# Position terms of an attention block: weights as windows of one small table on chip instead of tables from DRAM, heads interleaved, last terms in later turns

## The chip, the cores and the metric

The kernel runs on one core of a Trainium2 chip. The metric is the device time of one execution in microseconds (us). Before the change the median of three runs is 3649.41 us (3647.57 to 3650.12). PE is the matrix engine (PEld its weight loads), DVE the vector engine, ACT the scalar engine, POOL the GpSimd engine, and SP the engine that issues most of the DMAs. SBUF is the on-chip memory of 128 rows (partitions), PSUM the memory that PE writes its products to.

## The reference, cut to what matters

The program is a chain of four layers over an image of 48 x 48 positions with 768 channels: an attention block with an MLP, a spectral mixing layer, a scan layer, a second spectral layer. Only the attention block bears on the change:

```python
qkv = xn.reshape(B, H * W, C) @ qkv_w + qkv_b
...
attn = jnp.einsum('bqc,bkc->bqk', q * scale, k)
coords = jnp.arange(H)[:, None] - jnp.arange(H)[None, :] + (H - 1)
Rh = rel_pos_h[coords]
Rw = rel_pos_w[coords]
r_q = q.reshape(B * nh, H, W, hd)
rel_h = jnp.einsum('bhwc,hkc->bhwk', r_q, Rh)
rel_w = jnp.einsum('bhwc,wkc->bhwk', r_q, Rw)
attn = (attn.reshape(B * nh, H, W, H, W) + rel_h[:, :, :, :, None] + rel_w[:, :, :, None, :]).reshape(B * nh, H * W, H * W)
attn = jax.nn.softmax(attn, axis=-1)
out = jnp.einsum('bqk,bkc->bqc', attn, v)
```

There are 12 heads of 64 channels and 2304 positions. For a query in row h, `rel_h` is its 64 channels times 48 vectors, the 48 neighbouring rows of `rel_pos_h` (95 x 64) that start at a place which depends on h. `rel_w` is the same with the query's column w and `rel_pos_w`. So each of the 48 rows and 48 columns has its own 64 x 48 weights, and they are windows of one 64 x 95 array.

## The kernel before

Everything is float32. Two heads share the 128 rows of SBUF (`P`): head s of a pair has rows 64s to 64s+63. A matmul for both at once needs weights with zeros where the other head's channels stand. The host builds them: `relD` holds for each row and column a 128 x 96 block, columns 0 to 47 for the first head and 48 to 95 for the second, in groups of four positions (192 KB). The product has 96 rows, 0 to 47 of the first head and 48 to 95 of the second.

The qkv stage (`qkv_phase`, L241) works through the positions in three super-blocks of 768 (`sb`). For each it makes v (`v_rows`, L290, seven products by `rows_in_seven`) and then q and k for six pairs of heads (`q_and_k`, L328, seven products each with the weights `wqk`, 1344 KB, loaded from the scratch `wqk_d` by `load_qk`, L303). k, q and v go to scratch in DRAM.

The position terms of a super-block are a list of steps (`position_terms`, L439), 12 for rows (`rel_h`) and, except for the last super-block, 12 for columns (`rel_w`). Each step has a load and a run. `advance` (L492) keeps up to three loads ahead of the run; the runs are woven between the matmuls of q and k (L384) and of the next super-block's v (`between`, L502). A load issues one table of `relD` on SP's queue (`tables`, L433, four buffers); for rows it also has POOL copy q so that the positions of an image row stand side by side (`qh`, one buffer, L477 to L479). A run is four matmuls (L465, or L203 in `terms_w`) and `split_terms` (L186), in which ACT rounds the product to float32r and DVE subtracts for the rest. After four row steps, and after twelve column steps, two stores write the rows of the two heads to `rh_d` and `rw_d` (`store`, L446 to L448, on SP): 576 KB each for rh, 1728 KB each for rw.

The last super-block's column terms are made inside the attention stage, by the generator `last_terms_w` (L208): one load of q from scratch into part of `oT` (L217, 2304 KB), twelve products (L203), each with a table loaded three ahead in four buffers (L220 to L230), and stores at the end (L237). The attention stage (`attention_bounded`, L592) goes through 180 turns of three key tiles: scores (L629 products, L639 bias from `bt`), exp on ACT (L641), a running sum on DVE (L649), and every second turn the values (L660) of the two turns before; each six turns the row sums (L668), their reciprocal on DVE (L670) and the output (L676). Products of last terms share one PSUM bank (tag `rs`) with the row sums. Where they stand is written out by hand: one ahead of the values in the turns of `mid`, one after the values in the turns of `end` (L690):

```python
mid, end = {2, 3, 4, 5, 7, 8, 9, 10, 11, 13}, {8, 10}
```

Row sums come in turns 6 and 12. Beside the turns runs `weight_sums`, which loads weights of later stages on SP (`pw0b`, `pw1b`, ...), adds them on POOL (L134 to L137) and stores the sums; its tiles come from the pool of the exp results.

The order of SP's queue is the order of the program: an issue that waits for a free buffer holds all behind it. `relT`, the 64 x 2 x 95 array with both windows' sources, is also loaded (L413 to L415), for a bound on the scores (L422).

Of the kernel before, what the change touches and what calls it, by code (L numbers as in the profile page):

```python
# [20 lines left out]
P = 128  # L21
G = 48
# [170 lines left out]

def terms_w(nc, d, q, high, low, g, ps):


    R = 2 * G
    ps = ps[:R, :TB]
    pv = ps.rearrange("p (c b w h) -> p c b w h", c=NC, b=2, w=4)
    q6 = q.rearrange("p c b (j w h) -> p c b j w h", j=KJ, w=KTW)  # L200
    j, w0 = divmod(4 * g, KTW)
    for i in range(4):
        nc.tensor.matmul(pv[:, :, :, i, :], lhsT=d[:, i, :], rhs=q6[:, :, :, j, w0 + i, :], start=True, stop=True)  # L203
    cols = slice(j * P + w0 * KTH, j * P + (w0 + 4) * KTH)
    split_terms(nc, ps.rearrange("p (c b t) -> p c b t", c=NC, b=2), high[:R, :, :, cols], [(v[:R, :, :, cols], rows) for v, rows in low])


def last_terms_w(nc, oT, pw, pool, psum, q_d, rel_d, rw_d):  # L208
# [8 lines left out]
    nc.sync.dma_start(q.rearrange("p c b t -> p c (b t)"), q_d.rearrange("(c p) t -> p c t", p=P)[:, :, sb * ts : (sb + 1) * ts])  # L217
    tables = []

    def load(g):  # L220
        d = pool.tile([P, 4, 2 * G], F32, tag="relD", name=f"relDl_{g}", bufs=4)
        nc.sync.dma_start(d, rel_d[1, g])
        tables.append(d)

    for g in range(3):
        load(g)
    yield
    for g in range(G // 4):
        if g + 3 < G // 4:
            load(g + 3)  # L230
        terms_w(nc, tables.pop(0), q, high, low, g, psum(f"rwl_{g}"))
        if g == G // 4 - 1:
            for c0, c1 in ((0, 1), (1, NC2), (NC2, NC)):
                for s in range(2):
                    rows = slice(s * G, (s + 1) * G)
                    for n, v in enumerate((high[rows, c0:c1], low[c0 // NC2][0][rows, c0 % NC2 : (c1 - 1) % NC2 + 1])):
                        nc.sync.dma_start(rw_d[s, :, n, sb, c0 * ts : c1 * ts], v.bitcast(F32).rearrange("k c b t -> k (c b t)"))  # L237
        yield


def qkv_phase(tc, ident, x, qkv_w, qkv_b, relT, rel_d, ln_g, ln_b, q_d, k_d, v_d, rw_d, rh_d, wqk_d, wv_d, flag, home, ahead):  # L241

# [17 lines left out]
    with (  # L260
# [139 lines left out]
        with tc.tile_pool(name="qkv_v0", bufs=1, side="right") as vp:  # L400
# [11 lines left out]
            kb = kp.tile([P, NC], F32, tag="kb", name="kb")  # L412
            rel = qp.tile([P, 2, 2 * G - 1], F32, tag="rel", name="rel")  # L413
            for s in range(2):
                nc.sync.dma_start(rel[s * HD : (s + 1) * HD], relT)  # L415
            qms, kms = (qp.tile([P, NC, NSB], F32, tag=n, name=n) for n in ("qms", "kms"))
# [4 lines left out]
            rm = qp.tile([P, 2], F32, tag="rm", name="rm")  # L421
            V.tensor_reduce(rm, rel, axis=AX.X, op=ALU.max, apply_absolute_value=True)  # L422
            pz = qp.tile([P, 2, NC], F32, tag="pz", name="pz")
# [6 lines left out]
        with tc.tile_pool(name="qkv_o", bufs=1, side="right") as op:  # L430
            R = 2 * G

            def tables(which, g, n):  # L433

                d = qp.tile([P, 4, R], F32, tag="relD", name=f"relD_{which}_{g}_{n}", bufs=4)
                nc.sync.dma_start(d, rel_d[which, g])
                return d

            def position_terms(sb, q):  # L439
# [6 lines left out]
                def store(d, at, cols):  # L446
                    for s in range(2):
                        nc.sync.dma_start(d[s, :, :, sb, cols], at[s * G : (s + 1) * G].bitcast(F32).rearrange("k n c b t -> k n (c b t)"))  # L448

                def rel_w(g):  # L450
                    if g == 0:
                        tiles["rw"] = op.tile([P, KP, NC, 2, TB], F32R, tag="rw", name=f"rw_{sb}")
                    at = tiles["rw"]
                    terms_w(nc, tiles.pop(("w", g)), q, at[:, 0], [(at[:, 1], slice(0, NC))], g, pm.tile([P, 512], F32, tag="m", name=f"rw_{sb}_{g}"))
                    if g == G // 4 - 1:
                        store(rw_d, at, slice(0, NC * TS))

                def rel_h(cp, n, hh):

                    if (n, hh) == (0, 0):  # L460
                        tiles["rh"] = op.tile([P, KP, 2, 2, TB], F32R, tag="rh", name=f"rh_{sb}_{cp}")
                    (d, by_row), at = tiles.pop(("h", cp, n, hh)), tiles["rh"]
                    ps = pm.tile([P, 512], F32, tag="m", name=f"rh_{sb}_{cp}_{n}_{hh}")
                    for i in range(4):
                        nc.tensor.matmul(ps[:R, i * 2 * G : (i + 1) * 2 * G], lhsT=d[:, i, :], rhs=by_row[:, i], start=True, stop=True)  # L465
# [6 lines left out]
                def load(key, *args):  # L472
                    name = "_".join(str(k) for k in (sb, *key))
                    tiles[key] = tables(*args, name)
                    if key[0] == "h":
                        cp, n, hh = key[1:]
                        by_row = op.tile([P, 4, 2, KJ, KTW], F32, tag="qh", name=f"qh_{name}", bufs=1)  # L477
                        for c in range(2):
                            nc.gpsimd.tensor_copy(by_row[:, :, c], q6[:, 2 * cp + c, n, :, :, 4 * hh : 4 * hh + 4].rearrange("p j w h -> p h j w"))  # L479
                        tiles[key] = tiles[key], by_row.rearrange("p h c j w -> p h (c j w)")  # L480

                for cp in range(NC // 2):
                    for n in range(2):
                        for hh in range(2):
                            key = "h", cp, n, hh
                            steps.append((lambda key=key: load(key, 0, 2 * (2 * sb + key[2]) + key[3]), lambda key=key: rel_h(*key[1:])))
                for g in range(G // 4 if sb + 1 < NSB else 0):
                    steps.append((lambda g=g: load(("w", g), 1, g), lambda g=g: rel_w(g)))

# [102 lines left out]
def attention_bounded(tc, ahead, oT, last_terms, beside, load_next):  # L592
# [16 lines left out]
    with (  # L609
# [69 lines left out]
        other = beside(op, lambda name: pp.tile([P, 2, QB], F32, tag="p", name=name).rearrange("p a c -> p (a c)")[:, : 2 * TB].rearrange("p (a c) -> p a c", a=2))  # L679
        terms = last_terms(rp, lambda name: ps_v.tile([P, 512], F32, tag="rs", name=name))  # L680
        other_at = {15 + 28 * n // 5 for n in range(29)}
# [7 lines left out]

        mid, end = {2, 3, 4, 5, 7, 8, 9, 10, 11, 13}, {8, 10}  # L690
        for i in range(len(work) + 1):
# [37 lines left out]
def attention_any(tc, ident, oneh_d, q_d, k_d, v_d, rw_d, rh_d, oT, last_terms, beside, load_next):  # L729
# [5 lines left out]
    with tc.tile_pool(name="an_t", bufs=2) as op, tc.tile_pool(name="an_tp", bufs=2, space=PSUM) as pt:  # L735
        for _ in last_terms(op, lambda name: pt.tile([P, 512], F32, tag="t", name=name)):
            pass
# [652 lines left out]
def block_kernel(ctx: ExitStack, tc: tile.TileContext, a: dict):  # L1390
# [41 lines left out]

    qkv_phase(tc, ident, x, a["qkv_w"], a["qkv_b"], a["relT"], a["relD"], a["ln1_g"], a["ln1_b"], q_d, k_d, v_d, rw_d, rh_d, wqk_d, wv_d, flag, home, load_ahead)

# [10 lines left out]
    pw, pw_close = opened("pw", [P, 2, NC2, TB], "right")  # L1445
    last_terms = lambda pool, psum: last_terms_w(nc, oT, pw, pool, psum, q_d, a["relD"], rw_d)
    load_pw = lambda: nc.sync.dma_start(pw, ps_d[:, :2])
# [443 lines left out]
def laid_out(i):  # L1891
# [8 lines left out]

    rel = np.zeros((2, G, 2, HD, 2 * G), np.float32)
    for pos in range(G):
        for s in range(2):
            rel[:, pos, s, :, s * G : (s + 1) * G] = d["relT"].transpose(1, 0, 2)[:, :, G - 1 - pos : 2 * G - 1 - pos]
    d["relD"] = rel.reshape(2, G // 4, 4, P, 2 * G).transpose(0, 1, 3, 2, 4)
    for l, p in (("L1_", l1), ("L3_", l3)):
# [33 lines left out]
```

## Time and profile before

| What | Value |
|---|---|
| median of three runs | 3649.41 us |
| the profiled execution | 3647.4 us |
| its span, first to last instruction | 3645.6 us |
| PE busy | 3540.7 us, 97% |
| DVE, ACT, POOL busy | 1997.9, 1138.3, 681.1 us |
| PE's mean granted clock | 0.986 |
| qkv stage | 0 to about 474 us |
| attention | about 474 to about 1509 us |
| loads of tables (`relD`) | 72 of 192 KB |

Times in the profile are counted from the span's start. A row of the list of waits is: engine, line and tile, what it waited for, then total us, number of times, longest. A row of the timeline is: start, length, engine, line, operation, output and inputs, and in brackets the idle time ahead of it and what ended it. Where a row of DMA issues says "to landing", it counts from the issue to the last byte's arrival. The granted clock (PEclk) is a share of full speed.

### The profile page before, as it was taken

Reading aid. Unit: us, or ns where it says so; the run is one execution under the profiler, and the core shown is the slowest. Engines: PE = TensorE matmul, PEld = TensorE weight load, DVE = VectorE, ACT = ScalarE, POOL = GpSimd, SP = SyncE. Lnnn points to the kernel's source line nnn. Section 1 sums busy time; section 2 is a strip of 40 time slices with the busy share of each in tenths; the row PEclk is TensorE's granted clock in tenths of the full one; section 3 lists DMA queues with packets and bytes.
Section 4 is the critical chain, followed back from the end, with each engine's and each line's share of the span. In section 5 each row is a group of like instructions: output and inputs, shape, how many; then the busy total and the mean of one; then the engine's idle time right before and its main releaser. Section 6 shows DMA issues by size and latency. Waiting matters only on the chain.

```text
span 3645.6 us, 52273 instructions
## 1 busy us (share of the span) xinstructions
PE 3540.7 (97%) x20914; PEld 2173.6 (60%) x20914; DVE 1997.9 (55%) x3011; ACT 1138.3 (31%) x1731; POOL 681.1 (19%) x570
## 2 busy tenths in 40 slices
PE   7999989999999999999999999999999998999998
PEld 4656544444444444555555555555578777995685
DVE  6644346766677666655234324232245578994455
ACT  1222234444555445203101210121023365223341
POOL 3211101111111110250000000000023303971131
PEclk9999989999999999999999999999999999999999
DMA  7666665746455443344345334533444303113345
GB/s 256 225 221 203 213 191 152 186 138 170 135 151 141 126 122 97 94 147 152 110 126 181 111 108 128 155 111 112 151 123 112 99 23 103 33 30 95 97 115 156
DMA packets 267739, 491.83 MB, mean 135 GB/s; under 512 B 37182, under 2 KB 220286, under 8 KB 261280
## 3 DMA queue, kind: packets, MB, share of 16 engines
q1 hardware_dynamic: 257680, 467.45, 43.2%
q10 hardware_dynamic: 9808, 20.94, 1.6%
q8 instruction: 168, 2.75, 0.3%
q14 instruction: 83, 0.68, 0.1%
HBM read 344.69 MB, written 143.62 MB: 134 GB/s over the span
## 4 chain that ended last, share of the span: by engine, by line
PE 78%; DVE 3%; POOL 2%; DMA 2%; ACT 1%; issue 1%; SPq 0%; ACTq 0%; DVEq 0%; POOLq 0%
PE p L965 13%; PE p L1028 13%; PE av L660 12%; PE s L629 12%; PE c L1192 4%; PE s L639 3%; PE c L1285 3%; PE pj L169 2%; PE f_z L1600 2%; PE f_z L1599 2%; PE f_x L1564 2%; PE so L1370 2%; PE f_u L1614 2%; POOL t L1293 1%; PE f_w L1797 1%; PE f_o L1578 1%
## 5 line engine op out<-in xcount | busy, mean ns | idle before, releaser
L649 DVE TENSOR_TENSOR acc<-acc,p 128x928 f32<-128x928 f32 (+1 forms) x480 | 556.0, 1158 | 270.4 <-ACT p L641 229.6
L641 ACT ACTIVATE p<-s 128x928 f32<-128x928 f32 (+1 forms) x540 | 505.8, 939 | 495.2 <-PE s L639 470.4
L629 PE MATMUL s<-qt,kv 64*128 64x464 f32 (+1 forms) x2160 | 522.1, 559 | 5.6 <-ACT p L641 2.9
L1028 PE MATMUL p<-w,h 128*128 128x384 f32 x1512 | 492.7, 486 | 0.0
L660 PE MATMUL av<-p,kv 128*64 128x464 f32 (+1 forms) x2160 | 444.6, 556 | 0.0
L1028 PEld LDWEIGHTS p<-w,h 128*128 128x128 f32 x1512 | 286.1, 190 | 196.9
L639 PE MATMUL s<-bt,oneh 64*128 64x464 f32 (+1 forms) x1080 | 400.8, 731 | 1.2 <-DMA bt<-rh_d 1.2
L660 PEld LDWEIGHTS av<-p,kv 128*64 128x64 f32 x2160 | 147.5, 137 | 263.7 <-issue 252.5
L629 PEld LDWEIGHTS s<-qt,kv 64*128 64x128 f32 x2160 | 203.2, 187 | 162.6 <-issue 150.5
L965 PE MATMUL p<-x2nT,w 128*128 128x384 f32 x864 | 292.8, 488 | 3.2 <-issue 3.2
L355 PE MATMUL qk<-xnT,wqk 128*128 128x384 f32 x756 | 253.7, 493 | 9.9 <-DMA wqk<-wqk_d 9.9
L1285 PE MATMUL c<-H,bands 128*48 128x96 f32 x5632 | 243.8, 247 | 11.2 <-issue 11.0
L1285 PEld LDWEIGHTS c<-H,bands 128*48 128x48 f32 x5632 | 234.7, 123 | 20.6 <-issue 11.4
L965 PEld LDWEIGHTS p<-x2nT,w 128*128 128x128 f32 x864 | 164.9, 191 | 118.6 <-issue 4.9
L965 PE MATMUL p<-xT,w 128*128 128x384 f32 x648 | 220.8, 486 | 0.0
L1004 POOL TENSOR_TENSOR rr<-rr,ml_b 128x1152 f32<-128x1152 f32 x12 | 31.5, 2629 | 954.2 <-DMA rr<-xr_d 861.2
L355 PEld LDWEIGHTS qk<-xnT,wqk 128*128 128x128 f32 x756 | 143.3, 193 | 105.1 <-issue 10.2
L960 ACT ACTIVATE h<-h,ml_b 128x384 f32<-128x384 f32 x144 | 88.3, 614 | 345.9 <-DVE h L980 174.3
L1293 POOL TENSOR_TENSOR t<-s,c 128x768 f32<-128x768 f32 x80 | 144.7, 1832 | 179.0 <-DMA bands<-in_bands_dram 168.2
L965 PEld LDWEIGHTS p<-xT,w 128*128 128x128 f32 x648 | 123.1, 190 | 85.9
L639 PEld LDWEIGHTS s<-bt,oneh 64*128 64x128 f32 x1080 | 107.0, 188 | 106.5 <-issue 104.5
L1599 PE MATMUL f_z<-f_w,f_o 97*96 97x96 f32 x800 | 133.8, 249 | 0.0
(324 smaller groups left out, 4652.5 us busy)
## 6 DMA issues: line engine op xcount, KB each, us to landing
w<-w1s_d SPq DMA_DIRECT2D x36, 768.0 KB, 4.1
w<-w2s_d SPq DMA_DIRECT2D x36, 768.0 KB, 4.4
w<-w1s_d SPq DMA_DIRECT2D x36, 576.0 KB, 3.7
w<-in_mlp_w_dram SPq DMA_DIRECT2D x27, 768.0 KB, 4.5
wqk<-wqk_d SPq DMA_DIRECT2D x12, 1344.0 KB, 6.8
yu<-f_ys SPq DMA_DIRECT2D x24, 672.0 KB, 3.8
f_yt<-yu SPq DMA_DIRECT2D x20, 720.0 KB, 6.5
yu<-f_us SPq DMA_DIRECT2D x18, 720.0 KB, 4.8
```

Of the source, the lines that this page charges most:

```text
L355: nc.tensor.matmul(p[:, :TB], lhsT=w[:, n, c, :], rhs=ops[sb][n][:, c, :], start=c == 0, stop=c == NC2 - 1)
L629: nc.tensor.matmul(ps[:, s, :n], lhsT=keys[pr % 2][rows, kt * P : (kt + 1) * P], rhs=held(c)[rows, :n], start=True, stop=False)
L639: nc.tensor.matmul(ps[:, s, :n], lhsT=oneh[rows, b % 2, :], rhs=bts[b // 2][rows, j, :n], start=False, stop=True)
L641: nc.scalar.activation(p, ps[:, :, :n], AF.Exp)
L649: nc.vector.tensor_tensor(probs[c], probs[c], p, ALU.add)
L660: nc.tensor.matmul(avs[c][rows, : size(c)], lhsT=vals[pr % 2][:, kt, rows], rhs=p[:, s, :], start=kt == 0, stop=kt == NT - 1)
L965: nc.tensor.matmul(p[:, :TB], lhsT=w[n][:, c, :], rhs=rhs[n][:, c, :], start=c == 0, stop=c == NC2 - 1)
L1028: nc.tensor.matmul(ps[t][:, :TB], lhsT=hs[left, f][:, t * P : (t + 1) * P], rhs=wt[:, f % KW2, :], start=f == 0, stop=f == NF2 - 1)
L1192: nc.tensor.matmul(ps[:K, i, :n], lhsT=v[:, c, tok : tok + K], rhs=w[:, cc, c0 : c0 + n], start=cc == NC - 1, stop=cc == 0)
L1285: nc.tensor.matmul(ps[r0 : r0 + G, k // 4, cols], lhsT=bands[:, n - GC, i, :] if gr else bands0[:, n, i, :], rhs=H[:, n, :, d : d + NPR], ...
L1293: GP.tensor_tensor(t, sc[:, ch], c1[:, m0 : m0 + GC].unsqueeze(2).to_broadcast([P, GC, RR, NPR]), ALU.mult)
L1599: nc.tensor.matmul(out, lhsT=o1[:, j, 1:3, :].rearrange("c r h -> c (r h)"), rhs=w2t[:, b, 0, :], start=True, stop=False)
```

## The change

`load_windows` loads `relT` once, before the qkv stage, on ACT's queue, and makes from it one table `windows` of 128 x 2 x 95 x 2: the entries of head s stand in rows 64s to 64s+63 and in every other column, the rest is zero. The weights of a position are then 96 neighbouring columns of this table (`window`). `relD` and all its loads go, on the host too. The heads' columns are interleaved, so row 2k+s of a product belongs to head s, and each store takes every other row of 96 instead of 48 rows in a block. The copies of q for row terms have two buffers instead of one. The last terms come in turns 4 to 13 instead of 2 to 13 without 6 and 12.

```diff
+def load_windows(nc, pool, relT):
+    t = pool.tile([P, 2, 2 * G - 1, 2], F32, tag="windows", name="windows")
+    rel = pool.tile([P, 2, 2 * G - 1], F32, tag="rel", name="rel")
+    nc.vector.memset(t, 0.0)
+    for s in range(2):
+        rows = slice(s * HD, (s + 1) * HD)
+        nc.scalar.dma_start(rel[rows], relT)
+        nc.vector.tensor_copy(t[rows, :, :, s], rel[rows])
+    return t
+
+def window(t, which, pos):
+    return t[:, which, G - 1 - pos : 2 * G - 1 - pos, :].rearrange("p k s -> p (k s)")
...
-        nc.tensor.matmul(pv[:, :, :, i, :], lhsT=d[:, i, :], rhs=q6[:, :, :, j, w0 + i, :], start=True, stop=True)
+        nc.tensor.matmul(pv[:, :, :, i, :], lhsT=window(windows, 1, 4 * g + i), rhs=q6[:, :, :, j, w0 + i, :], start=True, stop=True)
...
-    def load(g):
-        d = pool.tile([P, 4, 2 * G], F32, tag="relD", name=f"relDl_{g}", bufs=4)
-        nc.sync.dma_start(d, rel_d[1, g])
-        tables.append(d)
...
-                    rows = slice(s * G, (s + 1) * G)
+                    rows = slice(s, 2 * G, 2)
...
-            rel = qp.tile([P, 2, 2 * G - 1], F32, tag="rel", name="rel")
-            for s in range(2):
-                nc.sync.dma_start(rel[s * HD : (s + 1) * HD], relT)
...
-            V.tensor_reduce(rm, rel, axis=AX.X, op=ALU.max, apply_absolute_value=True)
+            V.tensor_reduce(rm, windows.rearrange("p t k s -> p t (k s)"), axis=AX.X, op=ALU.max, apply_absolute_value=True)
...
-            def tables(which, g, n):
-                d = qp.tile([P, 4, R], F32, tag="relD", name=f"relD_{which}_{g}_{n}", bufs=4)
-                nc.sync.dma_start(d, rel_d[which, g])
-                return d
...
-                        nc.sync.dma_start(d[s, :, :, sb, cols], at[s * G : (s + 1) * G].bitcast(F32).rearrange("k n c b t -> k n (c b t)"))
+                        nc.sync.dma_start(d[s, :, :, sb, cols], at[s : 2 * G : 2].bitcast(F32).rearrange("k n c b t -> k n (c b t)"))
...
-                        nc.tensor.matmul(ps[:R, i * 2 * G : (i + 1) * 2 * G], lhsT=d[:, i, :], rhs=by_row[:, i], start=True, stop=True)
+                        nc.tensor.matmul(ps[:R, i * 2 * G : (i + 1) * 2 * G], lhsT=window(windows, 0, row + i), rhs=by_row[:, i], start=True, stop=True)
...
-                        by_row = op.tile([P, 4, 2, KJ, KTW], F32, tag="qh", name=f"qh_{name}", bufs=1)
+                    by_row = op.tile([P, 4, 2, KJ, KTW], F32, tag="qh", name=f"qh_{sb}_{cp}_{n}_{hh}", bufs=2)
...
-                    steps.append((lambda g=g: load(("w", g), 1, g), lambda g=g: rel_w(g)))
+                    steps.append((lambda: None, lambda g=g: rel_w(g)))
...
-        mid, end = {2, 3, 4, 5, 7, 8, 9, 10, 11, 13}, {8, 10}
+        mid, end = set(range(4, 14)), {8, 10}
...
+    windows = load_windows(nc, atc, a["relT"])
```

More of the change, by code (lines that the diff above doesn't have):

```diff
@@ L191, in split_terms, with terms_w @@
         nc.vector.tensor_tensor(part, ps[:, rows], high[:, rows].bitcast(F32), ALU.subtract)
-def terms_w(nc, d, q, high, low, g, ps):
+def load_windows(nc, pool, relT):
[9 more added lines that the diff above has]
+    return t[:, which, G - 1 - pos : 2 * G - 1 - pos, :].rearrange("p k s -> p (k s)")
+def terms_w(nc, windows, q, high, low, g, ps):
     R = 2 * G
@@ L202, in terms_w, with last_terms_w @@
     for i in range(4):
-        nc.tensor.matmul(pv[:, :, :, i, :], lhsT=d[:, i, :], rhs=q6[:, :, :, j, w0 + i, :], start=True, stop=True)
+        nc.tensor.matmul(pv[:, :, :, i, :], lhsT=window(windows, 1, 4 * g + i), rhs=q6[:, :, :, j, w0 + i, :], start=True, stop=True)
     cols = slice(j * P + w0 * KTH, j * P + (w0 + 4) * KTH)
     split_terms(nc, ps.rearrange("p (c b t) -> p c b t", c=NC, b=2), high[:R, :, :, cols], [(v[:R, :, :, cols], rows) for v, rows in low])
-def last_terms_w(nc, oT, pw, pool, psum, q_d, rel_d, rw_d):
+def last_terms_w(nc, oT, pw, windows, psum, q_d, rw_d):
     sb = NTB // 2 - 1
@@ L217, in last_terms_w @@
     nc.sync.dma_start(q.rearrange("p c b t -> p c (b t)"), q_d.rearrange("(c p) t -> p c t", p=P)[:, :, sb * ts : (sb + 1) * ts])
-    tables = []
-    def load(g):
-        d = pool.tile([P, 4, 2 * G], F32, tag="relD", name=f"relDl_{g}", bufs=4)
-        nc.sync.dma_start(d, rel_d[1, g])
-        tables.append(d)
-    for g in range(3):
-        load(g)
     yield
     for g in range(G // 4):
-        if g + 3 < G // 4:
-            load(g + 3)
-        terms_w(nc, tables.pop(0), q, high, low, g, psum(f"rwl_{g}"))
+        terms_w(nc, windows, q, high, low, g, psum(f"rwl_{g}"))
         if g == G // 4 - 1:
@@ L238, in last_terms_w, with qkv_phase @@
         yield
-def qkv_phase(tc, ident, x, qkv_w, qkv_b, relT, rel_d, ln_g, ln_b, q_d, k_d, v_d, rw_d, rh_d, wqk_d, wv_d, flag, home, ahead):
+def qkv_phase(tc, ident, x, qkv_w, qkv_b, windows, ln_g, ln_b, q_d, k_d, v_d, rw_d, rh_d, wqk_d, wv_d, flag, home, ahead):
     nc = tc.nc
@@ L453, in rel_w @@
                     at = tiles["rw"]
-                    terms_w(nc, tiles.pop(("w", g)), q, at[:, 0], [(at[:, 1], slice(0, NC))], g, pm.tile([P, 512], F32, tag="m", name=f"rw_{sb}_{g}"))
+                    terms_w(nc, windows, q, at[:, 0], [(at[:, 1], slice(0, NC))], g, pm.tile([P, 512], F32, tag="m", name=f"rw_{sb}_{g}"))
                     if g == G // 4 - 1:
@@ L461, in rel_h @@
                         tiles["rh"] = op.tile([P, KP, 2, 2, TB], F32R, tag="rh", name=f"rh_{sb}_{cp}")
-                    (d, by_row), at = tiles.pop(("h", cp, n, hh)), tiles["rh"]
+                    by_row, at = tiles.pop(("h", cp, n, hh)), tiles["rh"]
+                    row = 4 * (2 * (2 * sb + n) + hh)
                     ps = pm.tile([P, 512], F32, tag="m", name=f"rh_{sb}_{cp}_{n}_{hh}")
                     for i in range(4):
-                        nc.tensor.matmul(ps[:R, i * 2 * G : (i + 1) * 2 * G], lhsT=d[:, i, :], rhs=by_row[:, i], start=True, stop=True)
+                        nc.tensor.matmul(ps[:R, i * 2 * G : (i + 1) * 2 * G], lhsT=window(windows, 0, row + i), rhs=by_row[:, i], start=True, stop=True)
                     rows = at[:, :, :, n, :].rearrange("p s c (w h) -> p s c w h", h=KTH)
@@ L470, in rel_h, with side_by_side @@
                         store(rh_d, at, slice(2 * cp * TS, (2 * cp + 2) * TS))
[L472 to L476, printed above, removed]
-                        by_row = op.tile([P, 4, 2, KJ, KTW], F32, tag="qh", name=f"qh_{name}", bufs=1)
-                        for c in range(2):
-                            nc.gpsimd.tensor_copy(by_row[:, :, c], q6[:, 2 * cp + c, n, :, :, 4 * hh : 4 * hh + 4].rearrange("p j w h -> p h j w"))
-                        tiles[key] = tiles[key], by_row.rearrange("p h c j w -> p h (c j w)")
+                def side_by_side(cp, n, hh):
+                    by_row = op.tile([P, 4, 2, KJ, KTW], F32, tag="qh", name=f"qh_{sb}_{cp}_{n}_{hh}", bufs=2)
+                    for c in range(2):
+                        nc.gpsimd.tensor_copy(by_row[:, :, c], q6[:, 2 * cp + c, n, :, :, 4 * hh : 4 * hh + 4].rearrange("p j w h -> p h j w"))
+                    tiles["h", cp, n, hh] = by_row.rearrange("p h c j w -> p h (c j w)")
                 for cp in range(NC // 2):
@@ L485, in position_terms @@
                             key = "h", cp, n, hh
-                            steps.append((lambda key=key: load(key, 0, 2 * (2 * sb + key[2]) + key[3]), lambda key=key: rel_h(*key[1:])))
+                            steps.append((lambda key=key: side_by_side(*key[1:]), lambda key=key: rel_h(*key[1:])))
                 for g in range(G // 4 if sb + 1 < NSB else 0):
-                    steps.append((lambda g=g: load(("w", g), 1, g), lambda g=g: rel_w(g)))
+                    steps.append((lambda: None, lambda g=g: rel_w(g)))
             steps, ready = [], []
@@ L679, in attention_bounded @@
         other = beside(op, lambda name: pp.tile([P, 2, QB], F32, tag="p", name=name).rearrange("p a c -> p (a c)")[:, : 2 * TB].rearrange("p (a c) -> p a c", a=2))
-        terms = last_terms(rp, lambda name: ps_v.tile([P, 512], F32, tag="rs", name=name))
+        terms = last_terms(lambda name: ps_v.tile([P, 512], F32, tag="rs", name=name))
         other_at = {15 + 28 * n // 5 for n in range(29)}
@@ L735, in attention_any @@
     with tc.tile_pool(name="an_t", bufs=2) as op, tc.tile_pool(name="an_tp", bufs=2, space=PSUM) as pt:
-        for _ in last_terms(op, lambda name: pt.tile([P, 512], F32, tag="t", name=name)):
+        for _ in last_terms(lambda name: pt.tile([P, 512], F32, tag="t", name=name)):
             pass
@@ L1431, in load_ahead @@
         ahead.extend((loads, kvs, qbs, bts, ones, oneh))
-    qkv_phase(tc, ident, x, a["qkv_w"], a["qkv_b"], a["relT"], a["relD"], a["ln1_g"], a["ln1_b"], q_d, k_d, v_d, rw_d, rh_d, wqk_d, wv_d, flag, home, load_ahead)
+    windows = load_windows(nc, atc, a["relT"])
+    qkv_phase(tc, ident, x, a["qkv_w"], a["qkv_b"], windows, a["ln1_g"], a["ln1_b"], q_d, k_d, v_d, rw_d, rh_d, wqk_d, wv_d, flag, home, load_ahead)
     def opened(name, shape, side):
@@ L1445, in block_kernel @@
     pw, pw_close = opened("pw", [P, 2, NC2, TB], "right")
-    last_terms = lambda pool, psum: last_terms_w(nc, oT, pw, pool, psum, q_d, a["relD"], rw_d)
+    last_terms = lambda psum: last_terms_w(nc, oT, pw, windows, psum, q_d, rw_d)
     load_pw = lambda: nc.sync.dma_start(pw, ps_d[:, :2])
@@ L1899, in laid_out @@
     d["relT"] = np.stack([i[l0 + "rel_pos_h"][::-1].T, i[l0 + "rel_pos_w"][::-1].T], 1)
[L1901 to L1905, printed above, removed]
     for l, p in (("L1_", l1), ("L3_", l3)):
```

## The prediction

> **What bounds the kernel now.** The page comes first: TensorE (PE) is busy 3540.7 of 3645.6 us, so a change that leaves its work alone can only win part of the 105 us in which it idles, plus work done at a lowered clock. The second view is the list of what PE waited for:
>
> ```profile
> PE qk L355 <- DMA wqk<-wqk_d: 9.9, 2, 6.2
> ...
> PE rwl L203 <- DMA relDl<-in_relD_dram: 6.9, 1, 6.9
> ...
> PE rh L465 <- POOL qh_h L479: 3.3, 5, 1.2
> ...
> PE rw L203 <- DMA relD_w<-in_relD_dram: 1.7, 1, 1.7
> ```
>
> Two of these rows name a table that the change removes (6.9 and 1.7 us), one a copy that it gives a second buffer. The largest names the weights of q and k, which it does not touch. The timeline shows the 6.9 us at the start of attention:
>
> ```profile
> 486.86 0.41 SPq L217 DMA_DIRECT2D oT<-q_d  x1
> ...
> 487.39 1.50 SPq L222 DMA_DIRECT2D relDl<-in_relD_dram  x3
> ...
> 496.11 1.57 PE L203 MATMUL rwl<-oT,relDl 128*96 128x96 f32 x8 [6.92 <-DMA relDl<-in_relD_dram]
> ...
> 497.61 6.50 PE L660 MATMUL av<-p,kv 128*64 128x464 f32 x24
> ```
>
> The product in turn 2 needs the q columns (2304 KB, issued at 486.86) and a table queued behind them. After the wait PE runs slowly: eight products take 1.57 us where the later groups take 0.85, the values after them 6.5 where later turns take 4.82. The same timeline in the qkv stage, at the 6.2 us wait (L448 is the store of the w terms):
>
> ```profile
> 359.01 1.50 SPq L448 DMA_DIRECT2D rw_d<-rw  x2
> ...
> 365.64 3.93 SPq L305 DMA_DIRECT2D wqk<-wqk_d  x1
> ...
> 387.34 13.02 PE L355 MATMUL qk<-xnT,wqk 128*128 128x384 f32 x33 [6.21 <-DMA wqk<-wqk_d]
> ```
>
> A load of 1344 KB needs 21.7 us because it stands behind two stores of 1728 KB. Their rows in the answer on rw_d, and below them the one store of 4032 KB from all 128 partitions in the answer on wv_d:
>
> ```profile
> L448 SPq DMA_DIRECT2D rw_d<-rw x2: 622/726/831, 359.0 to 359.9; - x2
> DMA to landing us min/median/max: 13.8/17.2/20.6
> ```
> ```profile
> L428 SPq DMA_DIRECT2D wv_d<-wv x1: 331/331/331, 27.6 to 27.6; - x1
> DMA to landing us min/median/max: 11.0/11.0/11.0
> ```
>
> So 4032 KB from 128 rows land in 11.0 us, and 3456 KB from two blocks of 48 rows in 21.5 us (359.0 to 380.5). Stretches of 2 us say the same in the last column (GB/s), two inside the stores and one after them:
>
> ```profile
> 362.00:364.00 2.00, 2.00 (x8) 1.21 (x7) 1.03 (x3) 0.00 (x0) 1.49 (x1) 1.00 1.20 230
> 364.00:366.00 2.00, 2.00 (x8) 1.21 (x7) 0.68 (x2) 0.00 (x0) 1.13 (x1) 1.00 0.69 157
> ...
> 384.00:386.00 2.00, 0.00 (x0) 0.00 (x0) 0.00 (x0) 0.00 (x0) 0.00 (x0) 0.71 1.07 427
> ```
>
> The last wait that matters lies at 620 us, after the stores of the last w terms:
>
> ```profile
> 616.34 0.37 SPq L855 DMA_DIRECT2D pw1b<-in_proj_w_dram  x1
> ...
> 621.92 3.48 ACT L641 ACTIVATE p<-s 128x928 f32<-128x928 f32 x4 [3.88 <-POOL pw1p L136]
> ...
> 622.92 1.12 PE L629 MATMUL s<-qt,kv 64*128 64x464 f32 x4 [2.89 <-ACT p L641]
> ```
>
> [...] the first store landed after 13.8 us, behind a v store of 0.6 MB, the second some 7 us later. [...] idle from 381.1, clock 0.71 in 384 to 386, 0.50 next. [...] Tables and windows both have 96 (159 to 165 ns here)[...].
>
> **The change, part by part**, against this execution's 3647.4 us (span 3645.6 and 1.8 around it).
>
> 72 table loads of 192 KB go (36 for rows, 24 for w terms, 12 for the last), 14.2 MB, all on SP's queue.
>
> Last terms. The tables are gone, and the products move from turns 2, 3, ... to turns 4 to 13: each is eight matmul records on PE (0.85), a cast on ACT (0.47) and two subtractions on DVE (0.69), as before; their q load stays in turn 0 and their stores in turn 13, so SP loses twelve issues and is passed by nothing else. The q columns are what is late next: they were there by 496.1, since the product then ran. From 489.2 PE now has a turn of values (4.8) and two of scores (3.9 each) before it asks, at about 501.8, 5.7 us to spare. Gain 6.9, and the slow clock after it: 1.57 - 0.85 and 6.5 - 4.82, together 2.4. Sum 9.3.
>
> The table wait in the w terms at 341: 1.7. The second buffer for the copies: two waits of 0.35 around 166 us go, 0.7; those after 464 lie beside the chain last k store, q load, first scores, and win nothing.
>
> Stores with every other row. Before 359 and before 209 the queues had drained (60 and 98 GB/s in 354 to 358), so most removed tables free nothing there; the one issued at 358.36 does, 0.2 MB at 320 GB/s, 0.6 us. From 362 to 372 2.1 MB moved at 207 GB/s; at the 320 of the loads after it that is 6.5 us, so 3.5 saved[...]. The load of wqk lands 4.1 earlier. At 387.3 PE's wait falls from 6.2 to 2.1[...]: 4.1 + 2.2 (clock 0.5 to 0.6 over 387.3 to 392). At 238.2 the wait of 3.7 goes, with 1.7 of slow clock. Sum 11.7. Bounds of this term: 1.2 if only the table counts, 13.8 if both waits vanish.
>
> Start of attention. The first q load waits for the last k store (issued 464.37, landed near 471: 6.5 us, where the equal q stores have a median of 2.8) beside two rh stores of 576 KB[...]. I take 1.5 of the 0 to 3.7.
>
> The wait at 620. The twelve stores of last terms hold SP from 574.5 to 588.5; behind them come the loads of bias, of pw0b (593.41), POOL's sums, their store, three loads, and pw1b. A burst 3.5 us shorter pulls that chain by as much, and the wait of 2.9 and the slow clock after it (1.7) are just covered; I take 3.0 of 0 to 4.6.
>
> What it adds. ACT issues two loads of 47.5 KB at the start (ACT's first need is at 7.30); DVE clears 380 elements per row and makes two copies, each about the 0.34 us of the reduction over 190, before the first statistics, which waited for x until 5.53. Loads at an empty start land in 2.2 us (ln_g), so it is covered; if they take the 8.3 us of the old rel loads, all of it comes 4 us late. The reduction over 380 costs 0.2 more in DVE's gap at 30. I take -0.3. In turns 6 and 12 a product now stands before the row sums, which use its PSUM bank. The subtractions ended 2.4 us after a product's end in turn 5 (533.67 to 536.03), and the twelve values between take 2.41: cost 0, and up to 3 each without that cover; behind it on PE stand the row sums and twelve values, and DVE's reciprocal (3.06) waits for the sums. The other weights, terms and matmuls are unchanged in number and shape: 0. SP no longer stands at full table slots (140.9 and 29.9 us in its waits); what is behind them, x and wqk, waits for other slots or arrives early: 0.
>
> Sum: 9.3 + 1.7 + 0.7 + 11.7 + 1.5 + 3.0 - 0.3 = 27.6; 3647.4 - 27.6 = 3619.8. The profiled execution is 2.0 below the median of the runs, so 3622.
>
> **Rivals.** Tables only: the stores are no faster from other rows[...]. For it: the two kinds of store also differ in length of run (32 KB a row against 18) and in what ran beside them. Then 9.3 + 1.7 + 0.7 + 1.2 - 0.3 = 12.6 is left: 3637.
> More: [...]both wqk waits vanish (13.8 for 11.7) and PE keeps its clock at the start of attention, where it ran at 0.5 from 467 to 484; 2 + 2 + 6 more: 3612.
> The wait comes back: turns 6 and 12 stall, 3 us each, with tables only: 3643, no change that counts. Against it stand the 5.7 us and the 2.4 us above.
> Slower: stores that step over rows run below the others. Without the stores the change gains 11.4; slower by 7.3 us needs a loss of 18.7, 9.3 at each wqk wait, so 3456 KB in 30.8 us instead of 21.5 (115 GB/s against 165). At twice the time it costs 43: 3681. Against it: each row still leaves as runs of the same length.
>
> **How the numbers follow.** Forecast 0.55, tables only 0.25, more 0.10, wait back 0.06, slower 0.04. About 0.2% (7.3 us) is what a measurement of this kernel tells from no change; the first three are faster by more: 0.90, same 0.06, slower 0.04. The likeliest case's own range is 3616 to 3629; with tables only and its error it reaches to 3640, with the case of more and 1 us of error to 3611, and the late start's 4 us lies inside.
>
> **What would show it.** Right: no PE wait on a table or on q at rwl; rw stores landing in 8 to 15 us; wqk waits of at most 2.5 us in all; clock near 1.0 after 390 and 496. Wrong: rw stores still at 14 and 21 us (tables only); PE waiting at the row sums for DVE's subtraction; DVE waiting for rel before its first statistics.

## The result, and the profile after

The changed kernel takes 3622.83 us (median of four runs, 3617.49 to 3626.70), the kernel before in the same comparison 3649.76 us: a ratio of 0.993, with a 95% interval of 0.9918 to 0.9941. A second comparison, with five runs, gave 3620.76 against 3650.58 us, 0.9919 (0.9905 to 0.9932). The forecast was 3622 us.

The profiled execution of the changed kernel is the longest of the first four: 3626.7 us, span 3624.9 us, 3.9 us above the median. It gains 20.7 us of span on the profiled execution of before where the medians gain 26.9, so its numbers are read stage by stage below.

First the list of what PE waited for. The rows of before for the tables and for the copies are gone, and the one for the weights of q and k has shrunk from 9.9 to 0.3 us:

```profile
PE n_tp L98 <- DVE x L89: 18.0, 3, 11.7
...
PE s L623 <- DMA qt<-q_d: 5.7, 1, 5.7
...
PE s L623 <- ACT p L635: 2.0, 1, 2.0
...
PE qk L361 <- DMA wqk<-wqk_d: 0.3, 1, 0.3
```

The row with 5.7 us is new, but it is not 5.7 us lost: PE gets to the end of the qkv stage sooner and waits there for the same chain, last k store, q load, first scores. (With one buffer for the copies, below, this row is absent: PE waits for copies in that stretch instead, and the first scores come at 458.86 us, against 458.73 here.) The answer on `rw_d` around 350 us shows the stores of the w terms (the columns after the colon are the issue's own time and when it was issued), and the stretches of 2 us show what moved while they ran (last column GB/s, before it DMA share and PE's clock):

```profile
L445 SPq DMA_DIRECT2D rw_d<-rw x2: 559/580/602, 352.0 to 352.7; - x2
DMA to landing us min/median/max: 10.4/10.4/10.4
```
```profile
354.00:356.00 2.00, 2.00 (x8) 1.20 (x7) 1.02 (x2) 0.00 (x0) 0.46 (x1) 1.00 1.01 286
356.00:358.00 2.00, 2.00 (x8) 1.21 (x7) 0.56 (x1) 0.00 (x0) 2.00 (x1) 1.00 0.97 332
...
388.00:390.00 2.00, 2.00 (x7) 1.14 (x6) 1.04 (x2) 0.61 (x1) 0.00 (x0) 1.00 0.89 254
```

The answer lists one landing of the two, that of the first, 10.4 us; of the pair near 205 us it lists the second, 15.8 us. Before had 13.8 and 20.6 (the kernel with interleaved tables, below, lists both: 10.6 and 15.9). The rate inside the stores rose from 157 to 249 GB/s (362 to 372 us) to 286 to 332 (354 to 362 us). At 388 to 390 us PE is busy at a clock of 1.00, where before it had 0.50.

The start of attention in the timeline:

```profile
471.43 0.40 SPq L234 DMA_DIRECT2D oT<-q_d  x1
...
483.64 0.92 PE L220 MATMUL rwl<-oT,windows 128*96 128x96 f32 x8
484.49 4.89 PE L654 MATMUL av<-p,kv 128*64 128x464 f32 x24
```

The product starts with no wait, and the values behind it take 4.89 us instead of 6.50. The q columns landed 8.8 us after 471.43, at 480.2. A load of 96 columns of weights takes 159 to 165 ns from the windows (from the tables of the w terms, 159 to 165 before), so nothing in this trace shows a cost of the windows' start addresses.

Two places fall short of the forecast. One is the wait for an exponential's buffer that GpSimd's weight sums hold, which was to go; it now stands at 596 us, with 2.0 us where it had 2.89:

```profile
587.31 0.37 SPq L849 DMA_DIRECT2D pw1b<-in_proj_w_dram  x1
...
595.17 3.52 ACT L635 ACTIVATE p<-s 128x928 f32<-128x928 f32 x4 [3.00 <-POOL pw1p L136]
...
596.16 1.16 PE L623 MATMUL s<-qt,kv 64*128 64x464 f32 x4 [2.00 <-ACT p L635]
```

The other lies in code that the change does not touch, some 1400 us after the end of attention, in the scan layer. The wait for gathered rows in the list of before, and then of the changed kernel:

```profile
PE c L1701 <- DMA f_gt<-yu: 0.7, 1, 0.7
```
```profile
PE c L1696 <- DMA f_gt<-yu: 1.7, 1, 1.7
```

One microsecond more would be little, but the stretches of 2 us around it, before and changed, show that PE's clock (third number from the end) falls in the same place:

```profile
2874.00:2876.00 2.00, 1.25 (x11) 1.12 (x11) 0.61 (x2) 0.48 (x1) 2.00 (x1) 1.00 1.02 267
2876.00:2878.00 2.00, 1.93 (x14) 1.50 (x14) 1.77 (x2) 0.48 (x1) 1.94 (x3) 1.00 0.99 289
```
```profile
2848.00:2850.00 2.00, 0.46 (x5) 0.29 (x3) 1.15 (x2) 0.08 (x1) 2.00 (x1) 0.94 0.99 267
2850.00:2852.00 2.00, 1.86 (x9) 1.89 (x10) 1.68 (x3) 0.00 (x0) 1.94 (x3) 0.50 1.00 307
```

### The profile page after: what moved, and what is told of

Its sections match the earlier page's. It is cut to its first block, busy times and chain, and to the rows that moved or that the text cites. A ratio compares the mean times of both kernels' runs of the same rounds, so it can differ in the third digit from the quotient of the medians.

```text
span 3624.9 us, 52111 instructions
## 1 busy us (share of the span) xinstructions
PE 3539.1 (98%) x20914; PEld 2174.5 (60%) x20914; DVE 2002.9 (55%) x3014; ACT 1138.5 (31%) x1731; POOL 685.8 (19%) x570
## 4 chain that ended last, share of the span: by engine, by line
PE 87%; DVE 4%; DMA 3%; POOL 3%; ACT 2%; issue 1%; SPq 0%; ACTq 0%; DVEq 0%; POOLq 0%
PE p L959 14%; PE p L1022 13%; PE s L623 12%; PE av L654 12%; PE qk L361 6%; PE c L1186 4%; PE v L169 3%; PE s L633 3%; PE pj L169 2%; PE f_z L1594 2%; PE f_z L1595 2%; PE f_x L1559 2%; PE so L1364 2%; PE f_u L1609 2%; POOL t L1287 2%
## 5 line engine op out<-in xcount | busy, mean ns | idle before, releaser
L1279 PEld LDWEIGHTS c<-H,bands 128*48 128x48 f32 x5632 | 234.5, 123 | 20.7 <-issue 11.3
L169 PE MATMUL v<-wv,xnT 128*128 128x384 f32 x378 | 133.8, 499 | 0.6 <-DVE xnT L144 0.5
```

The source lines that it names most:

```text
L169: nc.tensor.matmul(p[:, :TB], lhsT=rhs[n][:, c, t * P : (t + 1) * P], rhs=w[:, c, :], start=c == 0, stop=c == NC2 - 1)
L1279: nc.tensor.matmul(ps[r0 : r0 + G, k // 4, cols], lhsT=bands[:, n - GC, i, :] if gr else bands0[:, n, i, :], rhs=H[:, n, :, d : d + NPR], ...
```

## The experiments

Each part was put into the kernel before alone or taken out of the changed kernel; two variants of the changed kernel stand at the end. The table gives for each kernel the median of its runs, its ratio to the kernel before in the same comparison (a statistic of the runs, not the quotient of the two medians), and from its profiled execution the length of three stages: to the first scores of attention, from there to the last row sums, and from there to the end of the span. The stages are those of one execution each.

| Kernel | median us | ratio (95%) | to first scores | attention | rest |
|---|---|---|---|---|---|
| before | 3649.76 | | 474.1 | 1031.4 | 2140.0 |
| changed | 3622.83 | 0.9930 (0.9918-0.9941) | 458.7 | 1020.1 | 2146.1 |
| changed, again | 3620.76 | 0.9919 (0.9905-0.9932) | 457.0 | 1016.5 | 2146.6 |
| interleaved alone | 3629.37 | 0.9940 (0.9924-0.9957) | 459.1 | 1026.5 | 2142.6 |
| w terms interleaved alone | 3633.19 | 0.9959 (0.9945-0.9973) | 461.6 | 1027.3 | 2142.5 |
| new turns alone | 3638.34 | 0.9967 (0.9956-0.9979) | 473.6 | 1019.3 | 2142.1 |
| changed, old turns | 3632.65 | 0.9945 (0.9929-0.9962) | 457.1 | 1030.1 | 2146.2 |
| both, tables kept | 3623.32 | 0.9925 (0.9908-0.9941) | 459.3 | 1017.3 | 2143.7 |
| both, tables kept, again | 3623.09 | 0.9919 (0.9906-0.9933) | 460.6 | 1017.1 | 2144.9 |
| changed, one copy buffer | 3619.01 | 0.9919 (0.9902-0.9935) | 458.9 | 1015.2 | 2146.5 |
| changed, wider pool | 3620.40 | 0.9926 (0.9909-0.9942) | 457.9 | 1016.4 | 2144.3 |
| same, windows on GpSimd | 3621.72 | 0.9918 (0.9904-0.9932) | 458.0 | 1015.8 | 2146.1 |

**Interleaving alone.** The tables still come from DRAM; only the order of their columns and the rows of the stores change.

```diff
-            rel[:, pos, s, :, s * G : (s + 1) * G] = ...
+            rel[:, pos, s, :, s::2] = ...
-   nc.sync.dma_start(d[s, :, :, sb, cols], at[s * G : (s + 1) * G]...)
+   nc.sync.dma_start(d[s, :, :, sb, cols], at[s : 2 * G : 2]...)
```

> The kernel before with one thing of the change alone: the heads' columns interleaved in the tables (which still come from DRAM) and the stores of all terms from every other row. My theory (the partitions of a store set its rate): both rw stores land within 16 us of their issue, the waits for wqk fall from 9.9 to about 3 us in all, the time by the terms of the prediction that stand for the stores less the one table (11.7 - 1.2), the start (1.5) and the wait at 620 us (3.0), so by 15 us, to about 3635 (3632 to 3640). Rival (the gain is that of the tables, which no longer queue ahead of the loads): rw stores still at 14 and 21 us, time 3648 to 3651.

Measured: 20.5 us faster, 3629.37, which is more than the expected 3632 to 3640. The rows for the rw stores near 352 us and for PE's waits in that kernel:

```profile
DMA to landing us min/median/max: 10.6/13.2/15.9
```
```profile
PE rwl L203 <- DMA relDl<-in_relD_dram: 7.9, 1, 7.9
...
PE qk L355 <- DMA wqk<-wqk_d: 0.9, 1, 0.9
```

The first scores come 15.0 us earlier, with every table still loaded, and the waits for wqk fall from 9.9 to 0.9 us. So most of the qkv stage's gain (15.4 and 17.1 us in the two executions of the changed kernel) is the stores'. The theory that the tables crowded the queue would have left this kernel at 3648 or more. The attention stage is also 4.9 us shorter, about what its wait near 620 us (2.9 us) and the slow clock after it (1.7) had cost: that wait doesn't appear in this execution.

**The heads apart.** To see that it is the partitions of a store that count, and not the order of issue or the step between rows, the second head's rows were moved to 64 to 111, still one unbroken block.

```diff
-                    rows = slice(s * G, (s + 1) * G)
+                    rows = slice(s * HD, s * HD + G)      # HD = 64
-   nc.sync.dma_start(d[s, ...], at[s * G : (s + 1) * G]...)
+   nc.sync.dma_start(d[s, ...], at[s * HD : s * HD + G]...)
```

> The kernel before with the heads' columns moved apart instead of interleaved: tables of 128 columns, head 0 in partitions 0 to 47 and head 1 in 64 to 111 of the terms, the rest zero. Stores are two unbroken blocks as before, tables are a third larger (256 KB, three buffers), and PE's weight loads are longer, so only the stores' landing is read, not the time. Theory of the partitions[...]: the second rw store near 359 us lands later than before's 20.6 us[...], and the first one at 13.8 as before[...]. Rival (only the step between rows matters, or the order of issue): 13.8 and 20.6 us as before.

The answer on `rw_d` around 388 us, and the waits:

```profile
L448 SPq DMA_DIRECT2D rw_d<-rw x2: 562/590/618, 387.6 to 388.3; - x2
DMA to landing us min/median/max: 28.1/28.1/28.1
```
```profile
PE qk L355 <- DMA wqk<-wqk_d: 24.7, 2, 14.1
```

The landing that is listed is that of the second store, 28.1 us (28.1 too for the pair near 219 us), the load of wqk behind it takes 29.5, and PE waits 24.7 us for such loads. The second store of the same size thus lands 15.9 us after its issue from every other row, 20.6 from rows 0 to 95 in halves, and 28.1 from rows 0 to 47 and 64 to 111. The last is later than 20.6, as the theory of the partitions has it; by the rival it would have stayed there. That the rows of a store set its time is shown by these three runs; what it is in the rows that does so is not. (The whole kernel took 3691.71 us in one run, but its weight loads and tables are longer too, seven loads of 128 columns 0.86 us where seven of 96 took 0.67, so that time says nothing about the stores alone.)

**The w terms alone.** Interleaving as above, but the terms along the rows stay in two blocks.

```diff
+   rows = slice(s, 2 * G, 2) if d is rw_d else slice(s * G, (s + 1) * G)
```

> The kernel before with interleaved columns and every other row's stores for the w terms alone; the terms along the rows stay in two blocks. Against the run with both interleaved (3629.4): by the prediction the terms along the rows are worth 1.5 us of the 16, at the start of attention: 3631. By the traces so far, where that start came only 0.6 us sooner after its k store: 3630. Rival (the many stores along the rows slow the loads in all of the stage): 3635 or more.

3633.19 us, but its runs spread from 3627.84 to 3637.58, and its interval overlaps that of the full interleaving, so the times don't settle it. The traces, one execution each, do in part: first scores at 461.55 instead of 459.13 us, 2.4 later. Of this, 1.8 us have built up by the last group of q and k (448.35 against 446.51; half of it is the wait for a table in the w terms, 1.5 us against 0.6), 0.6 us is the k store, from whose issue to the q load behind it 6.8 us pass (as before the change) instead of 6.2. So the row terms' stores are worth some 2.4 us, more of it inside the stage than at its end.

**New turns alone, and old turns in the changed kernel.**

```diff
-        mid, end = {2, 3, 4, 5, 7, 8, 9, 10, 11, 13}, {8, 10}
+        mid, end = set(range(4, 14)), {8, 10}
```

> The kernel before with the last terms in turns 4 to 13, all else kept, the tables too. My theory: by turn 4 both q and the first table have landed, so the wait of 6.9 us and the slow clock after it go, 9.3 us in all: 3640.5 (3638 to 3643). Rival (the wait comes back at turns 6 and 12, where a product now stands before the row sums): a row of PE waiting at the row sums of some 3 us each, 3643 to 3650. If the two parts of the last terms add up, this run and the one before it give the same 9 us.

> The changed kernel with the last terms back in turns 2, 3, 4, 5, 7 to 11 and 13. My theory (q is late, not only the table, since the changed trace has q land at about 480 us, where the product of turn 2 would be asked for at about 473): a wait of about 6 to 7 us for q at the first product, and 2 us of slow clock after it, so 8 to 9 us longer than the changed kernel, about 3631. Rival (the table was what held turn 2, and without tables the turns don't matter): no wait there, the same time within 2 us, about 3623.

Alone, the turns take 11.5 us off the kernel before (3638.34), and the attention stage is 12.1 us shorter. The price of 9.3 us was low; no row of PE waiting at the row sums appears. Taken back in the changed kernel they cost 9.8 to 11.9 us by medians (3632.65 against 3622.83 and 3620.76; the intervals of the ratios overlap), and the attention stage is 10.0 and 13.6 us longer. Its list of waits has

```profile
PE rwl L220 <- DMA oT<-q_d: 7.9, 1, 7.9
```

in a kernel that has no tables at all, and this is the 7.9 us of the kernel with interleaving alone, which waited there for `relDl`. Taking the table away without moving the turn thus shortens no wait: the q columns are as late.

**The tables.** The change less its removal of the tables: interleaved columns and new turns, tables loaded as before, one buffer for the copies.

> The kernel before with both other parts of the change, interleaved columns with every other row's stores and the new turns, but with the tables still loaded from DRAM and one buffer for the copies. So it is the change less its removal of the tables. My theory: the tables alone are worth 1.7 + 1.2 + 0.7 - 0.3 = 3.3 us, so this kernel takes about 3626 (3624 to 3630). Rival (14 MB less on SP's queue is what made the other parts work): at least half of the 27 us is missing, 3636 or more.

3623.32 us, half a microsecond from the changed kernel and just below the expected 3624 to 3630. Because the prediction had 3.3 us for it, both kernels then ran beside each other on one chip:

> The changed kernel, beside the next run on one chip, to see what the tables alone are worth. By the prediction's terms (table wait 1.7, table in the queue 1.2, second buffer 0.7, less 0.3 for the start) 3.3 us less than the kernel with the tables kept. By the traces so far: 0.6 us less at the start of attention, and then up to 5 us given back, at 596 us and near 2850 us, so between 1 us less and 4 us more.

> The kernel with both other parts of the change and the tables still loaded, beside the changed kernel on one chip: by the prediction's terms 3.3 us longer than that; by the traces so far between 4 us less and 1 us more. Its wait for the gathered rows near 2850 us is 1.2 us, under the 1.7 at which the changed kernel loses the clock.

3620.76 us (3620.49 to 3622.17) without tables, 3623.09 (3618.38 to 3625.10) with them. By medians 2.3 us, but the ratios to before are 0.9919 both times: the gain of the tables can't be told from none. The traces show two opposite parts. From PE's first transpose to the first scores the two executions without tables need 447.0 and 445.5 us, those with tables 448.8 and 449.4: 2.8 us won. From the last row sums to the end they need 2146.1 and 2146.6 instead of 2143.7 and 2144.9: 2.1 us lost. With 0.7 us at the start and 1.1 in attention lost as well, these four executions come out about even (about 1 us longer without tables, on average).

**One buffer for the copies.**

```diff
-   by_row = op.tile([P, 4, 2, KJ, KTW], F32, tag="qh", ..., bufs=2)
+   by_row = op.tile([P, 4, 2, KJ, KTW], F32, tag="qh", ..., bufs=1)
```

> The changed kernel with one buffer for the copies on GpSimd, as before. By the prediction's term the two waits near 166 us come back, 0.7 us, and those at the end of the stage lie beside the last k store: 3623.5. If all waits for copies that the kernel before shows count (3.3 us): 3626. If none: 3622.8.

The row of waits for copies is back, as before, and the time is 3619.01 us, below all three expected values and not longer than with two buffers:

```profile
PE rh L463 <- POOL qh L473: 3.3, 5, 1.2
```

The second buffer gains nothing that the times can show.

**The wait at 596 us, and the windows on GpSimd.**

```diff
-        tc.tile_pool(name="at_p", bufs=11) as pp,
+        tc.tile_pool(name="at_p", bufs=13) as pp,
```

> The changed kernel with 13 instead of 11 buffers in the pool of the exponentials, from which GpSimd's weight sums take theirs. My theory: the wait of PE at 596 us (2.0 us, and 1.7 at a lower clock) is for a buffer that the sums hold, so it goes: 2 to 3.3 us less, about 3620. Rival: the sums run as late as before and something else waits for them: no change.

The wait is gone from the profiled execution, and the time is 3620.40 us, which the intervals can't tell from the changed kernel. The changed kernel's second profiled execution shows why little is to be had: there the wait is missing without any wider pool. It is a matter between two chains, the exponentials and GpSimd's sums, that costs 2.0 us in one execution of the same kernel and nothing in the other.

```diff
-    nc.vector.memset(t, 0.0)
+    nc.gpsimd.memset(t, 0.0)
-        nc.vector.tensor_copy(t[rows, :, :, s], rel[rows])
+        nc.gpsimd.tensor_copy(t[rows, :, :, s], rel[rows])
```

> The changed kernel with 13 buffers in the pool of the exponentials and with the windows cleared and copied on GpSimd instead of VectorE. My theory: DVE's first statistics come at 5.5 instead of 6.4 us, as before, so PE's first transposes come 0.9 us sooner, and the wait at 596 us is gone: 0 to 0.9 us less than with the wider pool alone (3620.4), about 3620. If GpSimd's clearing and copying delay what it does for the first weights: PE's start is later than 11.7 us, 3621 or more.

The start of the changed kernel in the timeline, and of this one:

```profile
5.33 0.26 DVE L203 COPY windows<-rel 64x190 f32<-64x190 f32 x1 [1.62 <-DMA rel<-in_relT_dram]
5.62 0.55 DVE L425 TENSOR_REDUCE rm<-windows 128x2 f32<-128x380 f32 x1
6.43 1.02 DVE L73 BATCH_NORM_STATS2 ln_st<-x 128x6 f32<-128x384 f32 x2 [0.26 <-DMA x<-in_x_dram]
```
```profile
4.72 0.35 POOL L203 COPY windows<-rel 64x190 f32<-64x190 f32 x1 [1.02 <-DMA rel<-in_relT_dram]
5.74 1.02 DVE L73 BATCH_NORM_STATS2 ln_st<-x 128x6 f32<-128x384 f32 x2 [4.77 <-DMA x<-in_x_dram]
```

The first statistics come 0.7 us sooner than in that execution. But the wider pool alone, with the windows still on DVE, has them at 5.77 us and PE's first transposes at 11.03, where this kernel has 11.00, and the time is 3621.72 us: moving the work to GpSimd shows no gain. None of the three variants can be told from the changed kernel; no version here beats it beyond its interval.

## Why the prediction was right, point by point

**The sum.** The terms are of the right kind and the range held; that the sum came within 1.3 us of both medians is in part luck. By the table, the stage to the first scores won 15.4 us in the first profiled execution and 17.1 in the second; the terms for it (1.7 + 0.7 + 11.7 + 1.5 - 0.3) make 15.3. Attention won 11.3 and 14.9; its terms (9.3 + 3.0) make 12.3. The rest lost 6.1 and 6.6 us, where the prediction has 0. So the two executions gained 20.7 and 25.5 us where the sum says 27.6; the medians gained 26.9 and 29.8, since the profiled executions of the changed kernel were 3.9 and 1.2 us above their medians. Within the first stage, too, errors cancel: the stores gave more than their terms, the tables and the second buffer less.

**Stores with every other row (11.7).** That stores from such rows would land sooner was the author's estimate, as before has none of them. It held, and the term was too small. Interleaving alone brings the first scores 15.0 us forward, where 11.7 - 1.2 + 1.5 = 12.0 stood for it (the 1.2 is that of tables, which this kernel still loads); its table wait in the w terms fell with it, from 1.7 to 0.6 us. The step that kept 2.1 us of wait at 387 us was too careful: the load of wqk behind the stores landed 15.7 us after its issue instead of 21.7, so 6.0 earlier and not 4.1, and 0.3 us was left of both waits. The sign named for it, landings in 8 to 15 us, holds for the first store (10.4) and is just missed by the second (15.8). The rival "tables only" is out, the rival "slower stores" too. Of the rival "more" one half came, the waits for wqk, and one did not: PE's clock is still 0.50 from 458 to 466 us at the start of attention.

**Last terms (9.3).** Right that q is what is late next: the old turns in the changed kernel wait 7.9 us for it. The spare time was 3.4 us (480.2 to 483.64) and not 5.7: PE asked 12.2 us after the load's issue, where the steps of the prediction make 14.9 (486.86 to 501.8), and q landed 8.8 us after it. Most of that is a reading of the trace: the 3.9 us that the prediction takes for a turn of scores hold a product of the last terms (0.85), which the first turns no longer have. Two turns of scores took 6.1 us here (477.51 to 483.64), not 7.8. The size was 11.5 us alone and 9.8 to 11.9 when taken back. The feared stalls at turns 6 and 12 didn't come.

**Tables and second buffer (1.7 + 1.2 + 0.7).** The terms were too large. The 1.7 us wait fell to 0.6 (interleaved alone) and 0.9 (both, tables kept) where the tables stay but all stores are interleaved, so there was less for the tables' removal to gain; the second buffer gave nothing that the times show; and nothing shows the one table ahead of the stores as a gain of its own. Measured, for all three together: 2.8 us from PE's first transpose to the first scores, 2.3 us by medians of the whole, with none inside the interval.

**Start of attention (1.5).** 0.7 us: from the k store's issue to the q load behind it 6.8 us passed before and 6.1 after (449.34 to 455.46).

**The wait at 620 us (3.0).** The burst of twelve stores got 2.6 us shorter (14.0 to 11.4), but the chain to the weight sums moves forward with the scores that it delays, and the cover was as thin as "just covered" said: 2.0 us of wait in one execution of the changed kernel, none in another. With the new turns alone it is 3.5 us:

```profile
PE s L629 <- ACT p L641: 3.5, 1, 3.5
```

**Added work (-0.3).** PE's first transposes start at 11.03 to 11.69 us in the five profiles with windows made on DVE (mean 11.3), at 10.53 to 11.18 in six profiles with tables (mean 10.8): -0.5. The sign named for it, DVE waiting for rel ahead of its first statistics, did appear. What was missing in the working is the reduction: it no longer waits for a late load, so it moved from DVE's gap at 30 us to a place ahead of the statistics, 0.55 us. In the second execution of the changed kernel and in the one with the wider pool the statistics follow it at once (at 6.21 and 5.77 us); in the first they still wait 0.26 us for x.

**The step that failed** is one that wasn't in the sum: that what follows attention stays as it is. The scan layer took 932.9 us before from its first to its last `f_z` product, 938.1 and 939.8 after. In both executions a wait for gathered rows near 2850 us, 0.7 us before, is 1.7 and 1.6 us long, and PE then runs at a clock of 0.50 for some 6 us (2850 to 2856, and 2844 to 2850 in the second). By an estimate from these numbers, a clock of 0.50 over 6 us and a microsecond of wait are about 4 us of the 5 to 7. Over the whole layer PE idles 1.8 us more in the first execution than before, and the clock's shortfall, summed over stretches of 2 us, grows by 3.2; together that is about all of its 5.2.

Over the profiles this wait is 1.0 to 2.3 us with windows and at most 1.6 with tables, and the stage 937.6 to 940.5 against 932.9 to 938.0. It also grows the earlier attention ends, and the kernels with windows are mostly those that end it earliest; the old turns (windows, end of attention at 1487 us, rest 2146.2) and the interleaving alone (tables, 1486 us, rest 2142.6) point to the windows, the wider pool (windows, 1474 us, 2144.3) and the tables kept again (tables, 1478 us, 2144.9) do not, and each is one execution. What delays those rows is open.

## What to carry to other kernels

Before blaming the load that a wait names, look at what stands ahead of it in the same queue: here the cure for a wait on weights (9.9 us, 0.9 with the interleaving alone) was to store from other rows. A table taken out of a wait of several inputs shortened nothing here while the next input landed at about the same time (7.9 us of wait with the table and without): move the consumer, or bring both sooner. And a gain early in a long kernel can be trimmed where two chains meet with a microsecond to spare: here the rest of the kernel gave back 6.1 and 6.6 us, about 4 of them, by the estimate above, at waits of 1.7 and 1.6 us that a clock of 0.50 followed.

## What the runs showed of the hardware that was not expected

Some waits of PE of only 1.0 to 2.0 us were followed by a slower clock. After the 2.0 us at 596 us the clock was 0.74 in the next 2 us and 0.50 in the 2 us behind them, after the 1.7 us near 2850 us it was 0.50. At that same place waits of 1.2 us in two other executions (new turns alone, tables kept) kept it at 1.00, one of 1.3 us (tables kept again) lost it, 0.70 and 0.50 in 2846 to 2850, and so did one of 1.0 us (old turns, at 2857 us): 0.57 and 0.50 in 2858 to 2862. Elsewhere 1.7 us without work (new turns alone, in 2680 to 2690 us, a wait for `f_Z`) kept it at 1.00. That PE would keep its clock after a wait of 2.1 us, for which the prediction counted 2.2 us, was the author's estimate and doesn't hold of the 2.0 us at 596; and in these runs the length of the wait alone doesn't decide. What does is open.

The second of two stores of 1728 KB landed 15.9 (interleaved alone), 20.6 (before) or 28.1 us (heads apart) after its issue, with only the rows that they came from (and, in the last case, the size of the tables) changed. The scan layer far behind took 932.9 to 940.5 us in thirteen executions of eleven kernels with the same code for it.
